# Block sums of the first batch's features on GpSimd in place of VectorE, in a Perceiver block

## The chip, the cores and the metric

The kernel runs on one core of one Trainium2 chip. The metric is device time in microseconds (us), from one execution's start to its end; lower is better. A core has five engines that run side by side and meet only at semaphores: TensorE (PE, matmuls), VectorE (DVE), ScalarE (ACT), GpSimd (POOL) and SyncE (SP, which here only issues DMAs). GpSimd issues DMAs too, and while it does, or waits to do so, nothing behind in its queue runs.

## What is computed

Three residual steps on `x` (8 batches of 128 rows, 512 features), the first with a context of 2048 rows of 384 features for each batch:

```python
x = x + xattn(layernorm(x), ctx)      # q = x@Wq, k = ctx@Wk, v = ctx@Wv, 8 heads of 64,
                                      # softmax(q k^T / 8) v @ Wo + bo
x = x + attn(layernorm(x))            # q, k, v with biases, causal mask, softmax over the queries
x = x + ffn(layernorm(x))             # relu, rounded to an 8-bit float, second layer, rounded to fp16
```

The change touches the first step only: how the context is made ready for `ctx@Wk` and `ctx@Wv` of the first batch.

## The kernel before

**Matrix products with fewer multiplications.** Keys and values of a context half (1024 rows) are not computed as plain matmuls. The context is cut into 4 x 3 blocks (4 blocks of 256 rows, 3 of 128 features), the weights into 3 x 2, and 20 products of sums of blocks stand for the 24 plain ones. So sums must be made first: of the weights once (`sum_w`, 13 additions of 128x256, on VectorE, for Wk and for Wv), and of the context for each batch and half (`sum_half`, 20 additions or subtractions of 128x256). `x_both` holds the context's blocks for two halves, `m_both` eight further blocks for each half. `sum_half` writes partly into `m_both` and partly over the blocks of `x_both` themselves. `k_proj` (matmuls at L405) and `v_proj` (L428) then read both, and `block_product` gathers the 20 products, ScalarE taking copies (L325) and VectorE additions (L328, L331, L363).

**The first batch is special.** Its half 0 goes through plain matmuls for the keys (`k_plain`, L388), since TensorE would otherwise have nothing to do at the start; these read the blocks of `x_both` before they are overwritten. Only then is half 0 summed, for its values. Half 1 goes through `k_proj` and `v_proj`. For all later batches `next_half` loads a half and sums it on GpSimd; for the first batch both halves were summed on VectorE.

**The order at the start.** Lines 820 to 855 lay out the start. TensorE's, ScalarE's and (until the second step) VectorE's instructions keep the order of the program text; GpSimd's and SyncE's are placed by the scheduler of the tile framework. TensorE does, in this order: `k_plain(0)`, the beginning of `k_plain(1)`, the turns of four batches' normed rows (`q_turn`, L94, into `pt_q`), the rest of `k_plain(1)`, two blocks of the query projection (L472), the turns of the other four batches, the rest of the query projection, then `k_proj` of half 1, `v_proj` of half 0, and the scores. VectorE does the sums of Wk, statistics and normed rows of four batches (`q_norm`: L449, L451, L453, L455, with the root on ScalarE at L452), the same of the other four, half 1's sums, two small transposes of the self-attention's biases (L250), half 0's sums, the sums of Wv (L186 to L199), and then products of self-attention weights and biases (`dot`, L264), which need the biases spread over all partitions.

**The biases' rows.** `spread_biases` brings the two biases (`squares`, loaded by SyncE) into rows: VectorE turns 32x32 blocks (L250), GpSimd issues four DMAs for each bias to a line in DRAM (L252) and one that spreads the line over 128 partitions (L260, `row`). Behind them GpSimd's queue has the load of `bo` (L842, which takes over the memory of the first row and so waits for the products that read it), the additions of `bo` to `x_in` (L481, eight of 128x512), their store (`xd`, L482), and the third line (`u_line`, L252).

Of the kernel before, what the change touches and what calls it, by code (L numbers as in the profile page):

```python
# [25 lines left out]
def tile_perceiver_block(  # L26
# [21 lines left out]
    nc = tc.nc  # L48
# [89 lines left out]
    def x_block(b, h, at):  # L138
        return m_both[:, h, at] if isinstance(at, int) else x_both[:, h, at[1], at[0]]

    def sum_half(b, h, eng):

        for to, one, op, two in (
            (0, (2, 1), "-", (0, 1)),
            ((0, 0), (0, 2), "-", (0, 0)),
            ((0, 1), (0, 2), "-", (0, 1)),
            (1, (0, 2), "+", 0),
            (2, 1, "-", (1, 1)),
            (3, (3, 0), "-", (0, 0)),
            ((3, 1), (2, 1), "+", (3, 1)),  # L150
            (4, (3, 2), "-", (3, 1)),
            (5, (1, 1), "+", 4),
            ((1, 1), (1, 1), "-", (3, 1)),
            ((3, 1), 1, "-", (1, 0)),
            (7, (2, 0), "-", (1, 0)),
            (7, 7, "+", (0, 0)),
            (6, (1, 0), "-", (2, 2)),
            ((1, 0), (1, 2), "-", (1, 0)),
            ((1, 0), (1, 0), "-", 5),
            (0, 0, "-", 3),  # L160
            ((1, 1), (1, 1), "+", 3),
            ((2, 0), (2, 0), "-", (2, 2)),
            ((1, 2), (1, 2), "-", (2, 2)),
        ):
            eng.tensor_tensor(  # L165
                x_block(b, h, to), x_block(b, h, one), x_block(b, h, two),
                ALU.add if op == "+" else ALU.subtract,
            )
# [6 lines left out]
    def sum_w(halves, out, eng):  # L175

        def s(w):
            return out[:, WSLOT[w]]

        for w in WSLOT:  # L180
            if isinstance(w, tuple):
                nc.scalar.copy(s(w), halves(*w))
        b01, b11 = halves(0, 1), halves(1, 1)
        b00, b10, b20, b21 = (s(w) for w in ((0, 0), (1, 0), (2, 0), (2, 1)))
        add, sub = ALU.add, ALU.subtract
        eng.tensor_tensor(s(3), b11, b21, add)  # L186
        eng.tensor_tensor(s(1), s(3), b10, add)
        eng.tensor_tensor(s(11), s(1), b20, add)
        eng.tensor_tensor(s(2), b00, s(3), sub)
        eng.tensor_tensor(s(4), b00, b10, add)  # L190
        eng.tensor_tensor(s(4), s(4), b20, add)
        eng.tensor_tensor(s(5), b01, b21, add)
        eng.tensor_tensor(s(12), b10, s(5), sub)
        eng.tensor_tensor(s(18), b11, s(5), add)
        eng.tensor_tensor(s(15), b00, b01, add)
        eng.tensor_tensor(s(6), s(15), b21, add)
        eng.tensor_tensor(s(13), s(6), b20, add)

        eng.tensor_tensor(s(0), b21, s(1), sub)  # L199
# [57 lines left out]
    def spread_biases():  # L257
        for n in range(2):
            bias_rows.append(tmp.tile([P, D], F32, tag="t", name=f"row_{n}"))
            nc.gpsimd.dma_start(bias_rows[n], across(n))  # L260
# [205 lines left out]
    def q_proj(g, both, kept, blocks):  # L466

        xt, qt = both[:, 0], both[:, 1]
        for m in blocks:
            ps = bank(f"pq_{g}_{m}")  # L470
            for k in range(NK):
                nc.tensor.matmul(  # L472
                    ps, wq[:, k, ts(m, P)], xt[:, k, :],
                    start=(k == 0), stop=(k == NK - 1),
                )
            nc.scalar.copy(qt[:, m, :], ps)
            nc.sync.dma_start(kept[:, m, :], qt[:, m, :])
# [351 lines left out]
    warm = small.tile([P, 1], F32, tag="warm", name="warm")  # L829
    nc.scalar.activation(warm, eps, AF.Exp)  # L830
    q_proj(0, both[0], qds[0], range(2, NK))
    sum_half(0, 1, nc.vector)
    spread_biases()
    sum_half(0, 0, nc.vector)
    sum_w(lambda k, j: wv3[:, k, j, :], wv_sums, nc.vector)
    q_proj(1, both[1], qds[1], range(NK))
    load_q(0)
# [403 lines left out]
```

## Time and profile before

| what | value |
|---|---|
| median of 3 runs | 1086.88 us (1086.44 to 1087.02) |
| the profiled execution's own time | 1086.38 us |
| its span, first to last instruction | 1084.6 us |
| granted TensorE clock over the span | 1.000 |
| VectorE, sums of the first batch (L165), 40 of 128x256 | 27.73 to 43.38 us, 0.42 us each |
| GpSimd, the same line for later batches, 280 of 128x256 | 0.73 us each |
| GpSimd before 35.9 us | preparation to 1.4 us, then idle until VectorE's two transposes (L250) |
| GpSimd, the eight DMAs to the lines | 35.93 to 40.20 us |
| GpSimd, the two DMAs of the rows | issued 40.20 and 41.76 us |
| VectorE, first use of the rows (L264) | 50.35 us |

Times are those of one profiled execution, counted from its first instruction; the runs' median is 0.5 us above that execution. A line of the timeline gives start, length, engine, line in the program, operation, output and inputs by name, how many were merged, and in brackets the idle time of the engine before it with what ended it. PE stands for matmuls and PEld for the loads of their weights. Busy shares are averages over the whole span; the change lies in the first 45 us.

### The profile page before, as it was taken

The numbers are of one execution on the slowest core, as the hardware profiler recorded it, in microseconds if no ns is written. First come the engines' busy times: TensorE is split into PE (matmuls) and PEld (weight loads), VectorE is DVE, ScalarE is ACT, GpSimd is POOL, SyncE is SP. The second block draws the span as 40 slices with busy tenths as digits, with TensorE's granted clock in tenths as the row PEclk, the third lists the DMA queues.
The fourth block names the chain that finished last, engine by engine and source line by source line (L and its number), as shares of the span: only waits on it lengthen the run. The fifth ranks groups of instructions, "written<-read, shape, count | busy, mean of one in ns | idle before, by whom it ended". The sixth has DMA issues, their size and how long they took to land.

```text
span 1084.6 us, 15566 instructions
## 1 busy us (share of the span) xinstructions
PE 1077.8 (99%) x5638; PEld 708.4 (65%) x5638; DVE 759.1 (70%) x1639; ACT 352.4 (32%) x559; POOL 234.4 (22%) x350
## 2 busy tenths in 40 slices
PE   9999999999999999999999999999999999999998
PEld 5475774576467647755775577557746656768875
DVE  5876567778777877787688777777877657584333
ACT  3322133324332423432343324332433222323221
POOL 0144130350055005500540153035000312000000
PEclk9999999999999999999999999999999999999999
DMA  9476334553565456536544553555345745431001
GB/s 324 141 188 151 119 78 98 136 147 85 131 155 134 93 136 152 138 87 150 149 100 100 154 146 78 117 137 146 79 112 115 233 122 146 175 106 31 10 17 52
DMA packets 71853, 134.75 MB, mean 124 GB/s; under 512 B 28241, under 2 KB 36449, under 8 KB 70753
## 3 DMA queue, kind: packets, MB, share of 16 engines
q1 hardware_dynamic: 61120, 113.03, 40.8%
q0 software_dynamic: 3312, 11.03, 3.3%
q10 hardware_dynamic: 7344, 9.70, 3.1%
q8 instruction: 45, 0.74, 0.3%
q14 instruction: 32, 0.25, 0.1%
HBM read 54.01 MB, written 10.49 MB: 59 GB/s over the span
## 4 chain that ended last, share of the span: by engine, by line
PE 99%; DMA 0%; ACT 0%; DVE 0%; issue 0%; ACTq 0%
PE pv_z L428 22%; PE pk_z L405 21%; PE po L559 11%; PE sc L504 11%; PE pv_b L428 4%; PE pk_b L405 3%; PE ph_b L1066 3%; PE psk L715 3%; PE psv L759 3%; PE pf L1114 3%; PE pq L472 3%; PE py L642 3%; PE ph_c L1066 2%; PE ph_a L1066 2%; PE k L388 2%; PE ph L1018 1%
## 5 line engine op out<-in xcount | busy, mean ns | idle before, releaser
L528 ACT ACTIVATE p<-p,nm 128x2048 f32<-128x2048 f32 x64 | 128.2, 2003 | 274.9 <-DVE nm L516 185.9
L541 DVE STREAM_TRANSPOSE p<-p 128x512 f32<-128x512 f32 x256 | 158.9, 679 | 62.3 <-ACT p L528 62.1
L508 DVE TENSOR_SCALAR_CACHE_REDUCE p<-sc 128x512 f32<-128x512 f32 x256 | 159.0, 686 | 20.6 <-PE sc L504 18.9
L428 PE MATMUL pv_z<-wv_sums,x_both 128*128 128x256 f32 x640 | 157.9, 381 | 0.0
L165 POOL TENSOR_TENSOR m_both<-x_both 128x256 f32<-128x256 f32 x70 | 51.0, 729 | 490.5 <-DMA x_both<-in_ctx_t_dram 303.1
L405 PE MATMUL pk_z<-x_both,wk_sums 128*128 128x512 f32 (+1 forms) x320 | 149.2, 572 | 1.1 <-ACT kt L325 0.6
L428 PEld LDWEIGHTS pv_z<-wv_sums,x_both 128*128 128x128 f32 x640 | 120.5, 190 | 18.6 <-issue 2.2
L559 PEld LDWEIGHTS po<-pT,v 128*64 128x64 f32 x2048 | 111.2, 137 | 23.9 <-issue 23.2
L559 PE MATMUL po<-pT,v 128*64 128x128 f32 x2048 | 118.9, 274 | 0.1
L504 PE MATMUL sc<-kt,q 64*128 64x512 f32 x512 | 118.5, 602 | 0.0
L428 PE MATMUL pv_z<-wv_sums,m_both 128*128 128x256 f32 x448 | 107.3, 379 | 0.0
L405 PEld LDWEIGHTS pk_z<-x_both,wk_sums 128*128 128x128 f32 x320 | 59.2, 190 | 67.3 <-issue 54.5
L405 PE MATMUL pk_z<-m_both,wk_sums 128*128 128x512 f32 (+1 forms) x224 | 101.4, 568 | 0.0
L428 PEld LDWEIGHTS pv_z<-wv_sums,m_both 128*128 128x128 f32 x448 | 83.4, 190 | 12.6 <-issue 0.6
L504 PEld LDWEIGHTS sc<-kt,q 64*128 64x128 f32 x512 | 46.9, 186 | 65.6 <-issue 54.7
L325 ACT COPY v<-pv_z 128x512 f32<-128x512 f32 x112 | 62.9, 589 | 56.0 <-PE pv_z L428 55.5
L325 ACT COPY kt<-pk_z 128x512 f32<-128x512 f32 (+1 forms) x112 | 59.7, 562 | 58.0 <-PE pk_z L405 57.6
L405 PEld LDWEIGHTS pk_z<-m_both,wk_sums 128*128 128x128 f32 x224 | 40.8, 190 | 46.8 <-issue 35.1
L165 POOL TENSOR_TENSOR x_both<-x_both 128x256 f32<-128x256 f32 x98 | 70.1, 731 | 2.4 <-DMA x_both<-in_ctx_t_dram 2.3
L328 DVE TENSOR_TENSOR v<-pv_z,v 128x512 f32<-128x512 f32 x96 | 63.1, 684 | 5.5 <-PE pv_z L428 5.5
L328 DVE TENSOR_TENSOR kt<-pk_z,kt 128x512 f32<-128x512 f32 (+1 forms) x96 | 59.9, 650 | 5.8 <-PE pk_z L405 5.4
L328 DVE TENSOR_TENSOR v<-pv_b,v 128x512 f32<-128x512 f32 x48 | 32.9, 686 | 40.4 <-PE pv_b L428 40.4
(208 smaller groups left out, 1235.7 us busy)
## 6 DMA issues: line engine op xcount, KB each, us to landing
pT<-p SPq DMA_DIRECT2D x488, 128.0 KB, 2.3
x_both<-in_ctx_t_dram SPq DMA_DIRECT2D x45, 512.0 KB, 5.2
w<-in_w_t_dram SPq DMA_DIRECT2D x1, 4096.0 KB, 12.9
w2f<-in_w_t_dram SPq DMA_DIRECT2D x16, 256.0 KB, 2.7
pT<-p POOLq DMA_DIRECT2D x24, 128.0 KB, 4.1
x_in<-in_x_dram SPq DMA_DIRECT2D x8, 256.0 KB, 7.2
qd<-xq SPq DMA_DIRECT2D x8, 256.0 KB, 2.6
q<-qd SPq DMA_DIRECT2D x8, 256.0 KB, 3.9
```

Source lines behind the costliest of these rows:

```text
L165: eng.tensor_tensor(x_block(b, h, to), x_block(b, h, one), x_block(b, h, two), ALU.add if op == "+" else ALU.subtract,)
L325: nc.scalar.copy(outs[ij], views(ps))
L328: nc.vector.tensor_tensor(outs[to], views(ps), outs[other], op)
L405: nc.tensor.matmul(ps[:, : n * BK], wk_sums[:, WSLOT[WAT[r]], f2, :], x_block(b, hs, XAT[r]), start=start, stop=True, skip_group_check=True,)
L428: nc.tensor.matmul(ps[:, ts(t, 256)], x[:, ts(t, P)], wv_sums[:, WSLOT[WAT[r]], :], start=start and t == 0, stop=True, skip_group_check=True,)
L472: nc.tensor.matmul(ps, wq[:, k, ts(m, P)], xt[:, k, :], start=(k == 0), stop=(k == NK - 1),)
L504: nc.tensor.matmul(pair[i], q[r, :], kts[b, m // 2][r, m % 2, ts(n, 512)], start=True, stop=True)
L508: nc.vector.tensor_scalar(p[:, :, i].rearrange("p g (t i) -> p t g i", i=SQ)[:, ts(n, Q)], pair[i].rearrange("p (t g i) -> p t g i", g=Q, ...
L528: nc.scalar.activation(p[:, :, i], p[:, :, i], AF.Exp, bias=nms[b, m][:, i : i + 1], scale=SCALE, accum_out=sums[b][:, h : h + 1],)
L541: nc.vector.transpose(p[:, g, i], p[:, g, i])
L559: nc.tensor.matmul(pos[b][h * DH : (h + 1) * DH, ts(m, P)].rearrange("p (a i) -> p a i", a=Q), v[:, jt % 8, ts(2 * m + h, DH)], turned_[b, ...
L1066: nc.tensor.matmul(self.ps[to][:, ts(t, HR)], w[:, q, 2 * self.d + t], x[:, q], start=start and t == q == 0, stop=True, skip_group_check=True,
```

## The change

Two calls change their engine. `sum_half` itself, its blocks and their values stay as they are.

```diff
     q_proj(0, both[0], qds[0], range(2, NK))
-    sum_half(0, 1, nc.vector)
+    sum_half(0, 1, nc.gpsimd)
     spread_biases()
-    sum_half(0, 0, nc.vector)
+    sum_half(0, 0, nc.gpsimd)
     sum_w(lambda k, j: wv3[:, k, j, :], wv_sums, nc.vector)
```

In the built program VectorE has 40 instructions fewer, and the rest of its order is the same; TensorE's, ScalarE's and SyncE's orders are unchanged. GpSimd's queue after its preparation is now: five sums of half 0 that write only `m_both`, all twenty of half 1, ten more of half 0 (the ones that write over blocks that `k_plain` reads wait for those matmuls), the eight DMAs to the lines, the first row's DMA, the last five sums of half 0, the second row's DMA, and then as before. The sums wait for their loads, for each other, and for `k_plain`'s matmuls; nothing of VectorE's stands ahead of them.

## The prediction

> **What bounds the kernel now.** I read the page's busy row, then the chain of work that ended last, then the timeline of the first 100 us, engine by engine, because everything that the change touches lies there.
>
> ```profile
> PE 1077.8 (99%) x5638; PEld 708.4 (65%) x5638; DVE 759.1 (70%) x1639; ACT 352.4 (32%) x559; POOL 234.4 (22%) x350
> ...
> PE 99%; DMA 0%; ACT 0%; DVE 0%; issue 0%; ACTq 0%
> ```
>
> TensorE is busy from 1.5 us to the end and is 99% of the chain. Of the 6.8 us in which it isn't busy, the list of waits names only four in the first 110 us: 1.5 at the start, 0.6 and 0.5 in the first batch's key projections, 0.2 at the first load. So work taken from VectorE gains at most 0.5 us, and every us that TensorE waits early is added whole: after 100 us it idles 3.5 us in 984, so nothing later takes a delay up.
>
> The timeline of VectorE and TensorE shows how close the two stand where the change works (start, length, engine, line, tiles, count, idle before):
>
> ```profile
> 12.80 0.43 DVE L193 TENSOR_TENSOR wk_sums<-wk_sums 128x256 f32<-128x256 f32 x1
> ...
> 19.73 1.91 DVE L455 TENSOR_SCALAR xq<-x_in,qmv,qrs 128x512 f32<-128x512 f32 x4
> ...
> 22.78 1.91 PE L94 MATMUL pt_q<-ident,xq 128*128 128x128 f32 x16
> ...
> 25.90 1.91 DVE L455 TENSOR_SCALAR xq<-x_in,qmv,qrs 128x512 f32<-128x512 f32 x4
> ...
> 34.83 1.91 PE L94 MATMUL pt_q<-ident,xq 128*128 128x128 f32 x16
> ```
>
> VectorE's normed rows of x (xq, L455) are turned by TensorE (L94). The first tile of the first group has about 2.5 us in hand (ready about 20.3, used 22.78), the second group's about 8.4 (26.4, used 34.83).
>
> The last view is GpSimd and VectorE at 58 to 70 us, the only place in this execution where VectorE instructions with two SBUF inputs meet GpSimd arithmetic:
>
> ```profile
> 58.68 6.18 POOL L481 TENSOR_TENSOR x_in<-x_in,bo 128x512 f32<-128x512 f32 x5 [3.58 <-DMA bo<-in_xa_bo_dram]
> 65.37 3.72 POOL L481 TENSOR_TENSOR x_in<-x_in,bo 128x512 f32<-128x512 f32 x3
> ...
> 64.01 1.14 DVE L363 TENSOR_TENSOR kt<-kt 128x256 f32<-128x256 f32 x1
> 67.37 2.29 DVE L264 SCALAR_TENSOR_TENSOR unread<-w_sa,row 128x512 f32<-128x512 f32 x1
> ```
>
> L363 takes 0.42 elsewhere and ends here at 65.15, 0.29 after GpSimd's five adds (64.86). L264 takes 0.70 elsewhere and ends at 69.66, 0.57 after the three adds (69.09). At 1.24 us an add, the third began near 67.85, after L264 had asked: **VectorE did not get in between two GpSimd adds in a row.** Beside instructions that read PSUM (L328, L331, 0.42) no such stretch shows.
>
> **What is removed.** 40 adds on VectorE, 27.73 to 43.38, some 15.6 us. No TensorE wait is behind them, and the next VectorE work, the sums of wv (L186), waits until 45.17 for ScalarE's copies at 44.12. Gain: 0.
>
> **What is added.** 40 adds on GpSimd. A row of the same line shows the price: twenty of them from 96.33 to 109.4, 0.73 each, one begun every 0.685. In the changed program's order GpSimd has: five adds of half 0, twenty of half 1, ten of half 0, the eight line DMAs, the first row DMA, the last five adds of half 0, the second row DMA, then as before bo, the eight adds of L481, xd and the third line. It no longer waits for VectorE before them, only for the loads; so they start early.
>
> Step 1, at 12.35. Half 0 is landed by about 13.1 (last issue 6.5, 6.6 to landing), so five adds run 12.4 to 16. VectorE is then in the sums of wk (two SBUF inputs), with L193 to L199 still to come. By the rows above L193 asks at 12.80 and waits until about 16: +3.2. The bounds are 0 (VectorE's stream keeps the memory and GpSimd waits until 15.15) and 3.4; I take 3.2, since L193 waits for its predecessor's end and leaves a gap. This moves L449, the root on ScalarE and L455 from 19.73 to 22.9.
>
> Step 2, half 1. Its three loads are issued from 14.37 to 15.7 and take 8.0 to 9.3: they land at 22.4, 23.7 and 25.0. One add runs at 22.4, the next two can at 23.7, the rest at 25.0. L455's four (0.45 apart) ask at 22.9, wait for the first add's end at 23.1 and, if their stream is kept as GpSimd's was, end at 25.0. TensorE's first turn at 22.78 is 0.9 late.
>
> Step 3, **the step that decides**. From 25.0 GpSimd has 22 to 26 adds without a pause (the first that waits for the add just before it is the second of the ten after half 1's): 26 x 0.685 = 17.8, to 42.8. VectorE does the second group's statistics (one input), its root is taken on ScalarE, and L455 asks at 25.0 + (25.90 - 21.56) = 29.3. TENSOR_SCALAR from SBUF takes 0.54 for 512 elements where a two-input add takes 0.69; no row of before shows it beside GpSimd. Bounds: 0 (it needs nothing that GpSimd holds) and the whole stretch, 42.8 - 29.3 = 13.5. The nearest rows are L363 and L264, which waited a stretch out. Here a rule of the Trainium skill, page "SBUF — State Buffer", section "Who interferes with whom", bears: it lists tensor_scalar with two SBUF ports among what contends, and agrees; but it says that the loser waits for the other's whole *instruction*. By that, L455 would lose at most 0.73 four times, 2.9 of its 8.4 in hand, and TensorE nothing here. The L264 row passed over an instruction boundary, so I take the row: L455 starts at 42.8, the first tile is ready at 43.3, and TensorE's turn stands at 34.83: **+8.5**, with step 2's 0.9 in it. Without step 1 it would be 24 adds from 25.0, 41.5, and +7.2, up to 9.4 if the last three adds alternate with L455.
>
> Step 4. TensorE then idles some 7.6 us; no gap of before is above 1.5. The page "TensorE: Matmul & The Clock Gate", Part 1, says that an idle window of about 3.4 us halves the clock, until about 3.4 us of work. The trace grants 1.00 throughout and can't show it. Estimate from that page: half of 3.4, **+1.7**; by the trace alone 0.
>
> Step 5, the biases' rows. The line DMAs are now behind 35 adds, the second row DMA behind 40. With step 3: the last three of the ten end near 47.2 (behind L455's four), eight issues 4.3, row 0.6, five adds 3.4, row 0.6 and 4.1 to landing: about 60. L264 reads both rows at 50.35, moved by 10.2 to 60.6. So TensorE's delay covers it: 0. If that cover is gone (no step 3): ten adds end at 43.9, the second row lands at 56.6, L264 is 6.2 late; the idle 3.3 before L331 and 1.1 in hand there leave +1.9; and bo's load waits for L264, so the five adds of L481 come at 65 to 71, on top of L363, which moves to 65.9 and ends at 71.4: +4.4. Together +6.3.
>
> Behind those on GpSimd: xd must leave before pT's strips at 101.58, it lands at 75.3; the third line is read later still; TensorE takes half 1 at 57 and half 0 at 66.8 (sums done by 38 and 56). All 0.
>
> **Sum**: 8.5 + 1.7 = 10.2 on the profiled execution's 1086.38 = 1096.6. The median of the runs is 0.5 above that execution: **1097**.
>
> **Rivals.**
> A. GpSimd also gets in between L455's own instructions in step 2. Then the last two tiles of the first group wait while adds run on to the one that needs a TensorE matmul queued behind those very turns: about 25 adds from 24.05, to 41.2. TensorE's third turn, due at 23.74, comes at 41.7: +18, with the clock +20: 1107. For it: GpSimd's stream won twice. Against: L455's four have no waits between them, and only a stream that was running has been seen to win.
> B. They take turns, an instruction each, as the page says. Step 1 costs about the same; L455's first group runs 22.9 to 26.4, TensorE +2.2; adds end near 47.5, the second row lands at 60.2, L331 +3.2 more; L481's adds, which have no waits between them, cover L363 as in step 5, +4.4: 9.7, 1096.
> C. VectorE loses nothing to L165's adds; only step 5 without cover: +6.3, 1092.7. For it: L165's adds wait for each other by semaphore, L481's don't. Against: their spacing is 0.685 with and without those waits.
> D. Not slower: with neither step 1 nor 3, the rows come early enough. L481's adds then slide behind L363 and its 0.5 us wait goes: 1085.9 to 1086.5. It decides from the second row landing before 53.6 (50.35 + 3.3), that is 3 us earlier than 40 adds at 0.685 allow; so the adds would have to cost under 0.6. The 280 adds of before on GpSimd average 0.73.
>
> **Chances.** What a measurement of this kernel can tell from no change is about 0.2%, 2.2 us. Forecast 0.40 (1094 to 1099), A 0.25 (1103 to 1108), B 0.17, C 0.12, D 0.06. Slower 0.94, no change 0.04, faster 0.02. The range, 1091.5 to 1108, takes in A to C with their ends, and leaves out D and what I can't name.
>
> **What would show it.** Step 1: L193 with about 3 us in place of 0.43. Step 3: L455's second group with one instruction of some 10 us, ending with GpSimd's stretch, and TensorE idle from about 36 to 43 at L94. Step 4: a granted clock under 1 after that. Step 5: no wait at L331 beyond before's. A shows two long L455 in the first group and the idle at 24; C an L363 of 5 us. The prediction is wrong if L455 runs at 0.54 beside the adds.

## The result and the profile after

The changed kernel takes 1090.67 us (median of 6 runs, 1090.33 to 1090.90) against 1086.75 us for the kernel before in the same runs: a ratio of 1.0039, 95% interval 1.0029 to 1.0049, or 3.9 us slower. The prediction said slower, and 1097: the loss is 3.9 us where 10.2 were forecast, and the time lies just under the range (1091.5 to 1108). The profiled execution's span grew from 1084.6 to 1089.1 us.

The list of TensorE's waits in the first 105 us of the changed kernel (for whom, us in total, times, longest):

```profile
PE pk_z L405 <- DVE kt L331: 1.9, 2, 1.5
...
PE pv_z L428 <- DVE v L331: 1.1, 1, 1.1
PE pv_z L428 <- DVE v L328: 0.6, 1, 0.6
...
PE pt_q L94 <- ACT xq L95: 0.2, 1, 0.2
```

The long wait for xq at L94 that carried the forecast is not there. New are waits for VectorE in the key and value projections, between 62 and 83 us, when the last of the added sums (53.7) is already done. TensorE's timeline of the changed kernel shows where its delay grows:

```profile
23.16 1.65 PE L94 MATMUL pt_q<-ident,xq 128*128 128x128 f32 x12
...
35.82 1.91 PE L94 MATMUL pt_q<-ident,xq 128*128 128x128 f32 x16
...
64.16 0.67 PE L405 MATMUL pk_z<-x_both,wk_sums 128*128 128x256 f32 x2 [1.51 <-DVE kt L331]
...
68.86 1.89 PE L428 MATMUL pv_z<-wv_sums,x_both 128*128 128x256 f32 x8
...
78.71 1.10 PE L428 MATMUL pv_z<-wv_sums,x_both 128*128 128x256 f32 x4 [1.05 <-DVE v L331]
...
88.37 3.70 PE L504 MATMUL sc<-kt,q 64*128 64x512 f32 x16
```

In the kernel before, the second group of turns (L94) began at 34.83, and the other two were:

```profile
66.83 1.89 PE L428 MATMUL pv_z<-wv_sums,x_both 128*128 128x256 f32 x8
...
84.19 3.70 PE L504 MATMUL sc<-kt,q 64*128 64x512 f32 x16
```

So TensorE is 1.0 late at 35.8, 2.0 at the value projection and 4.2 at the scores. The second turns were not held; the rest was lost later.

VectorE and GpSimd of the changed kernel, from their timelines:

```profile
13.37 0.83 DVE L193 TENSOR_TENSOR wk_sums<-wk_sums 128x256 f32<-128x256 f32 x1
...
22.17 2.74 DVE L455 TENSOR_SCALAR xq<-x_in,qmv,qrs 128x512 f32<-128x512 f32 x4
...
28.14 3.65 DVE L455 TENSOR_SCALAR xq<-x_in,qmv,qrs 128x512 f32<-128x512 f32 x4
32.55 0.30 DVE L250 STREAM_TRANSPOSE squares<-squares 128x32 f32<-128x32 f32 x2 [0.76 <-DMA squares<-in_sa_bk_dram]
...
49.42 2.81 DVE L194 TENSOR_TENSOR wv_sums<-w_in,wv_sums 128x256 f32<-128x256 f32 x1
...
57.44 0.70 DVE L264 SCALAR_TENSOR_TENSOR unread<-row,row 128x512 f32<-128x512 f32 x1 [2.68 <-DMA row<-line]
...
66.75 0.42 DVE L363 TENSOR_TENSOR kt<-kt 128x256 f32<-128x256 f32 x1
...
71.86 1.58 DVE L264 SCALAR_TENSOR_TENSOR unread<-w_sa,row 128x512 f32<-128x512 f32 x1
73.54 4.16 DVE L264 SCALAR_TENSOR_TENSOR unread<-w_sa,row 128x512 f32<-128x512 f32 x1
```

```profile
45.00 4.26 POOL L252 DMA_DIRECT2D line<-squares  x8
49.25 0.59 POOL L260 DMA_DIRECT2D row<-line  x1
49.85 0.74 POOL L165 TENSOR_TENSOR x_both<-m_both,x_both 128x256 f32<-128x256 f32 x1
...
53.63 0.57 POOL L260 DMA_DIRECT2D row<-line  x1
61.67 0.54 POOL L842 DMA_DIRECT2D bo<-in_xa_bo_dram  x1 [7.47 <-DVE unread L264]
65.53 7.36 POOL L481 TENSOR_TENSOR x_in<-x_in,bo 128x512 f32<-128x512 f32 x5 [3.32 <-DMA bo<-in_xa_bo_dram]
72.83 0.55 POOL L482 DMA_DIRECT2D xd<-x_in  x1
73.41 3.72 POOL L481 TENSOR_TENSOR x_in<-x_in,bo 128x512 f32<-128x512 f32 x3
```

Two things are to be seen. First, two behaviours of the same pair of engines. Beside most of GpSimd's sums VectorE's instructions take about twice their time, one by one: L193 0.83 in place of 0.43, the second L455 group 3.65 in place of 1.91. But two instructions are shut out through several adds: L194 at 49.42 (2.81; 0.42 before) and L264 at 73.54 (4.16; 0.70 undisturbed). So these two engines meet not only at semaphores. Both stand beside adds that follow a DMA which GpSimd itself has just issued, the row at 49.25 and xd at 72.83. Second, the transposes (L250) are done at 32.85, but the lines are issued from 45.00 on, since 35 sums stand ahead of them; the second row is issued at 53.63, and L264 starts at 57.44, where it started at 50.35 before.

So two questions were open. When is VectorE shut out for a run of adds, and when for one add? And which part of the 3.9 us comes from the early sums, from the late rows, and from L264 behind xd?

### The profile page after: what moved, and what is told of

Its sections match the earlier page's. It is cut to its first block, busy times and chain, and to the rows that moved or that the text cites. A ratio compares the mean times of both kernels' runs of the same rounds, so it can differ in the third digit from the quotient of the medians.

```text
span 1089.1 us, 15575 instructions
## 1 busy us (share of the span) xinstructions
PE 1079.0 (99%) x5638; PEld 708.3 (65%) x5638; DVE 757.2 (70%) x1599; ACT 352.7 (32%) x559; POOL 265.6 (24%) x390
## 4 chain that ended last, share of the span: by engine, by line
PE 79%; DVE 1%; SPq 1%; ACT 0%; DMA 0%; issue 0%; DVEq 0%; ACTq 0%
PE pv_z L428 17%; PE pk_z L405 16%; PE po L559 9%; PE sc L504 9%; PE ph_b L1066 3%; PE pv_b L428 3%; PE pk_b L405 3%; PE psk L715 3%; PE psv L759 3%; PE pf L1114 3%; PE py L642 3%; PE ph_a L1066 2%; PE ph_c L1066 2%; PE ph L1018 1%; SPq L547 1%; PE pl L730 1%
## 5 line engine op out<-in xcount | busy, mean ns | idle before, releaser
L165 POOL TENSOR_TENSOR m_both<-x_both 128x256 f32<-128x256 f32 x80 | 59.6, 745 | 507.2 <-DMA x_both<-in_ctx_t_dram 441.6
L428 PEld LDWEIGHTS pv_z<-wv_sums,m_both 128*128 128x128 f32 x448 | 83.3, 190 | 13.9 <-DVE v L328 1.0
L165 POOL TENSOR_TENSOR x_both<-x_both 128x256 f32<-128x256 f32 x112 | 80.6, 739 | 2.0 <-DMA x_both<-in_ctx_t_dram 1.9
L328 DVE TENSOR_TENSOR v<-pv_z,v 128x512 f32<-128x512 f32 x96 | 63.1, 684 | 5.5 <-PE pv_z L428 5.5
L328 DVE TENSOR_TENSOR kt<-pk_z,kt 128x512 f32<-128x512 f32 (+1 forms) x96 | 60.0, 651 | 5.3 <-PE pk_z L405 5.1
L328 DVE TENSOR_TENSOR v<-pv_b,v 128x512 f32<-128x512 f32 x48 | 32.9, 686 | 39.0 <-PE pv_b L428 38.8
```

The source lines that it names most:

```text
L165: eng.tensor_tensor(x_block(b, h, to), x_block(b, h, one), x_block(b, h, two), ALU.add if op == "+" else ALU.subtract,)
L328: nc.vector.tensor_tensor(outs[to], views(ps), outs[other], op)
L428: nc.tensor.matmul(ps[:, ts(t, 256)], x[:, ts(t, P)], wv_sums[:, WSLOT[WAT[r]], :], start=start and t == 0, stop=True, skip_group_check=True,)
```

## The experiments

Times of the kernel before on the chips of these runs: medians 1086.14 to 1086.21. Ratios are to it, and an excess in us is a difference of medians from it.

### When a run of adds shuts VectorE out

A test kernel that has only GpSimd adds of 128x256 beside VectorE instructions, in eight sections, computes nothing of the block. One section, shortened:

```python
if dma: nc.gpsimd.dma_start(far, xs[:, 2])
for i in range(8):            # one: the result before it in section e, else xs[:, 0, :W]
    nc.gpsimd.tensor_tensor(pa[:, i], one, xs[:, 1, :W], ALU.add)
nc.vector.transpose(...)      # two (none in g and h), so that VectorE asks while the adds run
for i in range(10):
    nc.vector.tensor_tensor(...)   # or nc.vector.tensor_scalar(...), in c and d
```

> Nothing of the block is computed: eight short sections after one another set ten VectorE instructions beside eight GpSimd adds of 128x256, both from SBUF, and the time says nothing. a: adds alone, VectorE two-input adds that come about 1.3 us later. b: the same, the eight adds right behind a DMA that GpSimd issues. c, d: as a, b with VectorE tensor_scalar of 128x512. e: as b, each add waiting for the one before it. f: as b, but the adds wait until that DMA has landed. g, h: as b, a with VectorE there first. Theory 'behind a DMA': engines take turns, an instruction each (0.8 to 0.95 us each in place of 0.42), in a, c, h and f; in b, d and g one VectorE instruction waits until the whole run of adds is over (3 to 5 us); in e it gets in at the first gap. Rival 'the running stream keeps the memory': a and b alike, and c and d alike, one VectorE instruction of 3 to 5 us in each; in g and h the adds wait instead. Rival 'always turns': no VectorE instruction above 1 us anywhere, and the long ones of the changed kernel have another cause.

VectorE's ten instructions of a section (shortest, median and longest, in ns; a is without a DMA, b, d and g have one right ahead, e has one and each add waits for the last):

```profile
L89 DVE TENSOR_TENSOR va_a<-xs x10: 411/939/940, 7.6 to 14.0; 128x256 f32<-128x256 f32 x10
L89 DVE TENSOR_TENSOR va_b<-xs x10: 411/939/939, 20.3 to 27.3; 128x256 f32<-128x256 f32 x10
...
L91 DVE TENSOR_SCALAR va_d<-xs x10: 411/414/5203, 45.9 to 53.7; 128x512 f32<-128x512 f32 x10
L89 DVE TENSOR_TENSOR va_e<-xs x10: 411/938/940, 59.7 to 66.5; 128x256 f32<-128x256 f32 x10
...
L89 DVE TENSOR_TENSOR va_g<-xs x10: 410/412/6062, 89.0 to 97.7; 128x256 f32<-128x256 f32 x10
```

Without a DMA ahead the two take turns: 0.94 each while the adds run. So they do in c and h, which have none, and in f, whose adds wait until the DMA has landed (longest 0.95). Behind one, in d and g, a single VectorE instruction takes 5.2 or 6.1 us, and the rest run undisturbed at 0.41. In e, VectorE got in at the first gap between two adds, as expected. Only b was against the theory: it has a DMA right ahead, the first that GpSimd issued in that kernel, and there were turns. The second kernel of this kind repeats b and varies the rest (comments added here):

```python
section("a", "pool", "tt")            # DMA by GpSimd, tensor_tensor
section("b", "pool", "tt")
section("c", "pool", "tt", late=3)    # VectorE asks later
section("d", "pool", "ts", adds=20)   # tensor_scalar
section("e", "pool", "tt", adds=20, lag=2)   # each add waits for the one two before it
section("f", "sp", "tt")              # DMA by SyncE
section("h", "pool", "tt", cols=1)    # DMA of one column
section("i", "pool", "tt", late=1)    # VectorE asks earlier
```

> Computes nothing of the block: eight sections, each a run of 128x256 adds on GpSimd beside VectorE work with SBUF inputs. Theory (a run of adds right behind a DMA that GpSimd itself issues keeps VectorE out, one VectorE instruction of 5 to 14 us; otherwise turns at about 0.94): sections b and c (DMA, eight adds) hold, d and e (DMA, twenty adds; e with each add waiting for the one two before) hold for the run, h (DMA of one column) and i hold, f (DMA issued by SyncE) takes turns; a has the kernel's first GpSimd DMA, which in the earlier kernel took turns. Rival (a matter of the order of arrival, not of the DMA): f holds as often as b, or b and c take turns. Second rival (one-input TENSOR_SCALAR is the one that is held): only d holds.

```profile
L83 DVE TENSOR_TENSOR va_a<-xs x10: 413/938/940, 7.3 to 14.5; 128x256 f32<-128x256 f32 x10
...
L83 DVE TENSOR_TENSOR va_b<-xs x10: 409/411/5204, 20.6 to 28.4; 128x256 f32<-128x256 f32 x10
...
L83 DVE TENSOR_TENSOR va_e<-xs x10: 409/410/13365, 70.2 to 86.2; 128x256 f32<-128x256 f32 x10
L83 DVE TENSOR_TENSOR va_f<-xs x10: 411/939/940, 92.3 to 98.6; 128x256 f32<-128x256 f32 x10
```

b, c, h and i hold one instruction for 5.2, 4.6, 5.2 and 5.8 us, d and e for 13.4: until all eight or twenty adds are done. f, with the DMA on SyncE, takes turns. The size of the transfer doesn't matter (h moves one column), nor the operation (d has one input), nor a wait that is already met when the add comes up (e). Section a takes turns again: there GpSimd has 0.11 us of set-up between its first DMA and its first add (7.01 to 7.12), while behind the DMA of b the first add follows after 0.03. A gap may explain a, then, but not section b of the first test kernel, where the add began 0.01 after the DMA (19.94 to 19.95). Nor can a kernel's first DMA be the exception by itself: in the next run the store is GpSimd's first, and it holds. What let VectorE in there is open. Both rivals, as they were stated, are out.

### The same in the kernel: a DMA put ahead of half 1's sums

The change, with one small store of GpSimd's own ahead of half 1's second sum in the program text. It adds a store to a buffer that nothing reads. In GpSimd's queue three of half 1's sums came before it, and 24 sums without a gap behind it.

```diff
+            if ahead and to == (0, 0): eng.dma_start(ahead, x_block(b, h, (0, 2)))
             eng.tensor_tensor(
```

> The change, with one small store of its own issued by GpSimd just ahead of half 1's first add, so that a long run of adds stands right behind a GpSimd DMA. Theory (VectorE does not get in between adds that follow a GpSimd DMA without a gap): the second L455 group, which asks at about 28, is held until the stretch of adds ends (41 to 44), TensorE's turn L94 moves from 35.8 to about 43, and the run takes about 7 us more than the change, near 1097. Rival (engines take turns whatever stands ahead, or the hold is broken by the adds' waits on their loads or on each other): the second L455 group takes about 1.0 each as in the change, and the time is the change's plus at most 0.7, about 1091.

1095.85 us (four runs, 1095.04 to 1105.47), ratio 1.0109 (1.0074 to 1.0143): 9.7 over the kernel before, where the change alone loses 3.9. GpSimd, VectorE and TensorE of this kernel:

```profile
24.89 0.70 POOL L165 DMA_DIRECT2D ahead<-x_both  x1
...
42.11 0.79 POOL L166 TENSOR_TENSOR m_both<-x_both 128x256 f32<-128x256 f32 x1
```

```profile
28.47 16.46 DVE L455 TENSOR_SCALAR xq<-x_in,qmv,qrs 128x512 f32<-128x512 f32 x4
```

```profile
42.47 3.41 PE L94 MATMUL pt_q<-ident,xq 128*128 128x128 f32 x16 [6.16 <-DVE xq L455]
```

and the four L455 from 28 us on (shortest, median and longest, in ns):

```profile
L455 DVE TENSOR_SCALAR xq<-x_in,qmv,qrs x4: 943/946/13855, 28.5 to 44.0; 128x512 f32<-128x512 f32 x4
```

The first L455 of the second group is held for 13.86 us, until GpSimd has its first gap (0.08 us before the add at 42.11, which waits for its predecessor); from there the three others take turns at 0.94. TensorE idles 6.16 us and then does its 16 turns in 3.41 in place of 1.91. Two stretches (length, then busy us of PE, PEld, DVE, ACT and POOL with counts in parentheses, granted clock, DMA share, GB/s):

```profile
36.00:42.00 6.00, 0.30 (x1) 0.00 (x0) 6.00 (x1) 0.59 (x1) 6.00 (x9) 0.72 0.12 44
42.00:46.00 4.00, 3.53 (x17) 3.02 (x18) 3.13 (x6) 1.84 (x4) 3.05 (x6) 0.57 0.00 0
```

The granted clock (third number from the end) is 0.72 in the idle stretch and 0.57 in the first 4 us of work after it. Read in stretches of 1 us, it is 1.00 to 38, 0.50 from 39 to 45 and 1.00 from 46. So the prediction's steps 3 and 4 come about here, caused by one DMA that the changed kernel does not have there: when the turns are done, TensorE is 9.15 us behind the kernel before (45.72 against 36.57), where 10.2 were forecast. Step 5's cover holds as well: TensorE's wait for L331 is 0.5, as in the kernel before.

Two controls show that neither a GpSimd DMA farther ahead nor the transfer does it. In the first, the same store is put ahead of half 0's five sums; GpSimd issued it at 7.07, and the loads' waits lie between it and all sums. In the second it stays in its place, but SyncE issues it.

```diff
-            if ahead and to == (0, 0): eng.dma_start(ahead, x_block(b, h, (0, 2)))
+            if ahead and (to, op) == (0, "-") and two != 3: eng.dma_start(ahead, x_block(b, 0, (0, 2)))
```

> The change with the same small store issued by GpSimd, but ahead of the five first adds of half 0, so that it stands right before a run of five and the waits for half 1's loads come between it and the long run. Theory (the hold lasts only from a GpSimd DMA to the first gap in GpSimd's queue): the second L455 group takes turns as in the change (about 3.7 for its four), TensorE has no long wait at L94, and the time is the change's, 1090.2 to 1091.5; at 12.3 one VectorE instruction of the sums of wk may be held about 3 us. Rival (one GpSimd DMA more anywhere ahead of the adds costs it): about 1096 as with the store in front of the long run.

```diff
-            if ahead and to == (0, 0): eng.dma_start(ahead, x_block(b, h, (0, 2)))
+            if ahead and to == (0, 0): nc.sync.dma_start(ahead, x_block(b, h, (0, 2)))
```

> The change with the same small store at the same place ahead of half 1's first add of x blocks, but issued by SyncE. Theory (it is GpSimd's own issuing that shuts VectorE out, not the transfer): the second L455 group takes turns, 3.7 for four, and the time is the change's, 1090.2 to 1091.0. Rival (the transfer's traffic, or a change in the order of the adds, did it): one L455 of over 10 us and about 1096.

1090.61 (1.0040, 1.0025 to 1.0055) and 1090.62 (1.0038, 1.0024 to 1.0053): both the change's own loss. The second L455 group takes turns, 3.66 for its four in each. The 3 us at 12.3 that the first expectation allowed for did not come: the store was 4.6 us past by then.

But these controls also show that a DMA right ahead does not always bring a hold. In both, the five sums behind the first row's DMA follow it after 0.02 us, as in the changed kernel, where L194 was shut out for 2.81; here they take turns. In the first control:

```profile
49.09 0.95 DVE L194 TENSOR_TENSOR wv_sums<-w_in,wv_sums 128x256 f32<-128x256 f32 x1
49.10 0.60 POOL L260 DMA_DIRECT2D row<-line  x1
...
49.72 0.89 POOL L166 TENSOR_TENSOR x_both<-m_both,x_both 128x256 f32<-128x256 f32 x1
49.96 0.94 DVE L195 TENSOR_TENSOR wv_sums<-wv_sums,w_in 128x256 f32<-128x256 f32 x1
```

Here L194 ended (50.04) before GpSimd's first add did (50.61). All twenty holds in the profiles of this case, in twelve kernels, stand at adds that follow a GpSimd DMA within 0.03 us; these two runs of sums, and section b of the first test kernel, follow one as closely and took turns. What decides between the two is not shown.

### Where the 3.9 us come from

Only the five early sums of half 0 on GpSimd, everything else as before:

```diff
-            eng.tensor_tensor(
+            (nc.gpsimd if b == h == 0 and (to in (0, 1, 2, 6) or (to, op) == (7, "-")) and two != 3 else eng).tensor_tensor(
```

> The kernel before, with only the first five sums of half 0 on GpSimd; the prediction's step 1 alone. Theory (turns of one instruction each): L192 to L196 take about 0.94 in place of 0.43, the first L455 group begins about 2.4 late (22.2 in place of 19.73) at its old 0.45 each, TensorE's first turn of xq waits 0.2 to 0.9, so +0.4 to +1.0, ratio 1.0004 to 1.0009, and no further loss after 40 us. The prediction's own step 1 (VectorE shut out until GpSimd's stretch ends): one instruction of about 3 us and +0.9. Rival (the adds cost nothing by themselves): within 0.2 of before.

1085.97 us, ratio 0.9996 (0.9988 to 1.0005). VectorE's first L455 group begins at 22.13, 2.4 late as expected, yet TensorE does not wait for it: in this execution its own key projection ended 0.75 later (23.53), which is not explained; with half 1 alone, where no sum runs before 21 us, it ended 0.5 later (23.27). The rival "they cost nothing" is the nearer one.

Half 1 alone on GpSimd, and half 0 alone:

```diff
 sum_half(0, 1, nc.gpsimd)
 spread_biases()
-sum_half(0, 0, nc.gpsimd)
+sum_half(0, 0, nc.vector)
```

> Half 1 alone on GpSimd, half 0 stays on VectorE. Theory (three terms: 1.0 us because the first xq are late, 1.0 because the biases' rows are late, 2.1 because L264 stands behind L481's adds): no add runs before 22.4, so the first xq are ready near 21.6 as before; twenty adds end near 38, the line DMAs near 42, the second row lands near 47.5, before its use at 50.35. All three terms go: ratio 1.000, 1086.9 us, and L455's second group takes about 3.6 us without TensorE waiting. Rival 'stream keeps the memory': L455's second group waits until about 38, TensorE 3 us at 34.8: 1090. Rival 'any add on GpSimd costs by contention': half of the 4 us, 1088.8.

```diff
-sum_half(0, 1, nc.gpsimd)
+sum_half(0, 1, nc.vector)
 spread_biases()
 sum_half(0, 0, nc.gpsimd)
```

> Half 0 alone on GpSimd, half 1 back on VectorE. Five adds of half 0 still run from about 12.3 to 16.5 beside the sums of wk, fifteen more follow without half 1's twenty among them, so the line DMAs wait only for VectorE's transposes as in the kernel before. Theory (three separate losses: xq about 1.0 late, rows late about 1.0, an L264 held behind the xd store about 2): the first loss stays, the second goes, the third depends on where the xd store falls; with half 1 alone costing nothing (1085.74), half 0 alone gives +0.4 to +1.2 over the kernel before, ratio 1.0004 to 1.0011, first xq group about 2.4 late (22.2), no long wait for L331 in the trace. Rival (each half costs its share of 3.9): +2, ratio 1.0018.

1085.74 (0.9996, 0.9988 to 1.0004) and 1086.55 (1.0004, 0.9996 to 1.0012). Neither half costs anything measurable; the two together cost 3.9. The loss is no sum of shares. With half 1 alone the lines leave GpSimd at 37.42, with half 0 alone at 41.43, with both at 45.00, and the second row at 44.49, 48.00 and 53.63: it seems that only both together carry it past what the slack ahead of L331 absorbs. With half 0 alone, L264 is also held behind xd (3.72 at 67.91), and no TensorE wait follows. So in these runs that hold costs only where the rows are late already.

The whole change, with the lines' and rows' DMAs on SyncE:

```diff
-            nc.gpsimd.dma_start(line[:, ts(a, SQ)], squares[a * SQ : a * SQ + NK, n])
+            (nc.gpsimd if n == 2 else nc.sync).dma_start(line[:, ts(a, SQ)], squares[a * SQ : a * SQ + NK, n])
-            nc.gpsimd.dma_start(bias_rows[n], across(n))
+            nc.sync.dma_start(bias_rows[n], across(n))
```

> Both halves on GpSimd as in the change, but the eight line DMAs and two row DMAs of the biases are issued by SyncE. Theory: the rows land near 40, L264 stands where it did, L331 and L481 too; only the late first xq stay: +1.0, 1087.9 us, ratio 1.001; no wait of TensorE at L331 beyond 0.5. Rival 'contention of the adds makes it all': the rows' place doesn't matter, 1090.5. Rival 'it is the queue alone': 1086.9, and the 1.0 at the first turn goes with it.

1087.20 (1.0008, 1.0000 to 1.0016). All forty sums are still on GpSimd, and 1.0 of the 3.9 us is left (0 to 1.7 by the interval). TensorE's waits in the first 105 us:

```profile
PE pk_z L405 <- ACT kt L325: 0.6, 1, 0.6
...
PE pt_q L94 <- DVE xq L455: 0.2, 1, 0.2
```

The waits for L331 and L328 are gone, although L264 is held here too (3.73 at 68.08).

The change, with L481's eight adds in one run and one xd store behind them all:

```diff
-        nc.gpsimd.dma_start(xd[:, ts(g, GB), :], x_in[:, ts(g, GB), :])
+        if g: nc.gpsimd.dma_start(xd, x_in)
```

> The change, with L481's eight adds in one run and one store of x_in behind them in place of two stores, one after four batches each. Theory 'behind a DMA': no adds stand behind a store, so all L264 beside them take at most about 1.6 us each, the v additions come 2.5 us earlier and TensorE's 1.05 and 0.59 at v_proj go: 1089.0 us, ratio 1.002. Rival 'the running stream keeps the memory': the second L264 waits for the whole run, to about 76.5, and v comes later still: 1091.7. Rival 'always turns, and the 4.2 us had another cause': 1090.7, with a long L264 still there.

1088.14 (1.0026, 1.0015 to 1.0037; seven runs, five of 1087.5 to 1088.9 and two of 1090.7 and 1090.8). Beside these eight adds L264 takes 1.58, 1.59 and 1.58, a turn each, where the changed kernel had 4.16; the waits in the value projection are gone, and those for L331 in the key projections are left (1.6 in three).

So the late rows explain about 3 of the 3.9 us (what moving their DMAs takes away). Part of it comes about through the hold behind xd that they push into the value projection, but how much is not settled. By medians the run with one store loses 2.0 less than the change, but the two intervals overlap. And how the late rows show varies: in the two controls, at the same total and with the same hold behind xd (4.2 us each), the value projection waited only 0.8, but the key projection 2.6 and 2.1 in one piece for L331. The late rows and the hold are not separate terms: the first makes the second matter. The rest, 0 to 1.7, was not split up.

## Why the prediction was wrong, step by step

**What bounds the kernel** was right: TensorE, and every early wait is added whole. TensorE's idle time (span less busy) grew by 3.3 us of the 4.5 by which the span did.

That the kernel gets slower was forecast from step 3 and came true through step 5: the direction was right for another reason.

**The removal** was costed at nothing. No run speaks against it. The price of an added sum was right as well (0.72 to 0.73 where undisturbed), though its row shows nineteen sums from 96.33, not twenty.

**Step 1** took L193 as held for 3.2 us. The five sums and L192 to L196 took turns instead, 0.83 to 0.95 each, and VectorE lost 2.4 (L449 at 17.51; 15.07 before). The size was nearly right by the wrong mechanism; alone it costs nothing measurable.

**Step 2** put TensorE's first turns 0.9 late; they are 0.4 late (23.16), and with a 0.24 us wait inside, TensorE is 1.0 late at the end of them; 0.4 of it was there before they began, since the key projection ended later (23.32 against 22.94).

**Step 3 failed**, and it held 8.5 of the 10.2 us. It put the second L455 group at one wait of 13.5 us until GpSimd's stretch ends; in the changed kernel its four instructions took turns with the sums, 3.65 us in all, and TensorE did not wait for them. The prediction read the L264 row of the kernel before, which passed over an instruction boundary, as what GpSimd adds do to VectorE. That row stood right behind xd's DMA, with adds from 65.37:

```profile
64.80 0.55 POOL L482 DMA_DIRECT2D xd<-x_in  x1
```

No hold in these profiles comes without such a DMA, and half 1's sums had none ahead. L363, the other row, had waited for the rest of one add only, and could not tell the two readings apart. The Trainium skill, page "SBUF — State Buffer", section "Who interferes with whom", says that the loser waits for the whole instruction; the prediction weighed this and took the row. In the changed kernel the section's sentence is what happened (L455 1.05, 0.94, 0.94, 0.94), and the row's behaviour appears only behind a DMA of GpSimd's own (2.81, 4.16). Nothing had tied the one row to the place where it was to be used. With a DMA put there, step 3 comes true nearly to the number: L455 held to 42.3 (forecast 42.8), TensorE's turns at 42.47 (forecast 43.3).

**Step 4** had nothing to act on in the changed kernel: no idle stretch, clock 1.00. With the store ahead of half 1's sums it did: 6.16 us of idle time, then 1.5 us more for the 16 turns, against an estimate of 1.7 from the Trainium skill, page "TensorE: Matmul & The Clock Gate", Part 1. The trace agrees in kind and nearly in size: the clock was at half within 2.7 us of the last matmul (36.30) and whole again about 3.5 us after the first turn (42.47), where the page has about 3.4 for each.

**Step 5** stood at nothing because step 3 was to cover it, with +6.3 if the cover went. The cover went. The second row was forecast to land at 56.6 (the terms written there add up to 56.9) and landed at 56.94; L264 to be 6.2 late, and was 7.1. Of the two terms, +1.9 at L331 measured 1.0 (TensorE 1.0 late before the key projection, 2.0 behind it). The +4.4 at L363 did not come: there were 3.32 us between bo's DMA and the adds, and L363 took 0.42. L264 behind xd took its place, with 2.2 us of new delay in the value projection. So 3.2 where 6.3 was written.

**Rivals.** The mechanism is that of B in its turns and of C in its path: turns of one instruction, no long stall, and the rows late without cover. Both priced L481's adds at 4.4 by the same misread row, the largest single excess in B's 1096 and C's 1092.7. The delays as measured, 1.0 with steps 1 and 2 and 3.2 with step 5, add up to the 4.2 by which the scores are late.

## What to carry to other kernels

A row that carries most of a forecast has to be looked at with its neighbours: ask what the same engine did just before it, and whether that also holds in the place it is to be used for. Work moved to an engine that also issues DMAs delays everything queued behind it there: list those DMAs first, with their slack, because here about 3 of the 3.9 us went with the rows that stood behind the sums. And where sums must share the stage with VectorE, keep GpSimd's own DMAs from standing right ahead of a long run of arithmetic, or issue them from SyncE: here one such store cost 5.2 us when GpSimd issued it, and nothing measurable when SyncE did.

## What the runs showed of the hardware

- A run of GpSimd adds that follows a GpSimd DMA within 0.03 us can keep VectorE instructions with SBUF inputs out until the run's first gap: 5.2 us for eight adds, 13.4 us for twenty, 13.9 us in the kernel. GpSimd's adds of 128x256 then keep their 0.71 to 0.75. A gap of 0.08 us was enough to end it (before the add at 42.11 with the store ahead, and at 52.02 in the changed kernel).
- It does not always do so: behind the first row's DMA in the two controls, and in section b of the first test kernel, the two took turns.
- Without the DMA, or with SyncE issuing it, both take turns, 0.94 for VectorE (0.41 alone) and 0.90 for GpSimd (0.72 alone).
- Where there is a hold, it makes no difference here whether the VectorE instruction has one SBUF input (tensor_scalar, 13.36 us) or two (tensor_tensor, 13.37 us).
- What in GpSimd causes the hold was not tried; the runs show where it came and when it ended.
